# Attention and feed-forward kernel: input kept in the output sums, last two pairs plain, first products by 128 tokens

## The chip, the cores and the metric

The kernel runs on one core of one Trainium2 chip. The metric is the device time in microseconds; a run's time is compared with the median of the kernel's runs. TensorE (PE in the profile) does the matrix products, with its weight loads listed apart as PEld; VectorE is DVE, ScalarE is ACT, GpSimd is POOL, and SyncE (SP) issues all DMA transfers from one queue.

## The reference

One layer on 1024 tokens of width 512, in float32: attention with 32 heads of width 128 and a causal mask, then a feed-forward part of three square layers whose weights are signs (+1 or -1), each after a normalisation and each added to its input.

```python
x = x + attn(layernorm(x), wq, wkv, wo)
x = x + ffn(layernorm(x), k0, s0, k1, s1, k2, s2)

# attn: S = 1024, H = 32, DN = DV = 128, DQ = 192
q = (y @ wq).reshape(S, H, DQ)[..., :DN]
k = (y @ wkv)[:, : H * DN];  v = (y @ wkv)[:, H * DN : 2 * H * DN]   # by heads
scores = where(causal, q @ k.T * DQ ** -0.5, -1e30)
out = (softmax(scores) @ v).reshape(S, H * DV) @ wo

# ffn, D = 512, ei(y) scales the last fifth of y by -4 before the product
h = 2 * relu(s0 * (x @ sign(k0)))
h = 2 * relu(s1 * (ei(h) @ sign(k1)))
out = s2 * (ei(h) @ sign(k2))
```

## The kernel before, in words

**Layout.** Tokens lie in 8 tiles of 128 (`NT`), four to a half (`TPB`, halves of 512 tokens). The normalised input is transposed into `xnT` (features by tokens) by TensorE (`transposed`, L209, tile `ptx_a`), one tile after the other: statistics (L193, L194), square root on ScalarE (L196), reciprocal (L198), normalisation on VectorE (L203), four transposes, copy on ScalarE (L216).

**Pairs.** The 32 heads go in 16 pairs (`g`, 0 to 15). Every matmul but the transposes is recorded at L66, so this text tells them apart by the tile that they write. The projections of a pair and the output products are done in seven products of half-size blocks instead of eight (a Strassen scheme): `products` makes q, k and v of a pair in the banks `X`, `Y` and `Z`, from token sums `T` (`token_sums`, L229 to L232) and weight sums that POOL makes (`sums_of`, L244 to L247). Only q and k of pair 0 are made plainly, by `qk_plain`, at the start: for each half of the tokens, for q and k and both heads, four matmuls of 512 columns into one bank, copied out by ScalarE (L273).

**Heads.** For each query tile (`qt`, here "step"), `probabilities` makes the scores (`sc_qt`, one bank pair, so a score waits until the one before it has been read), VectorE takes the maximum and adds the mask (L465), ScalarE the exponential (L476), VectorE the reciprocal of the sum (L480), ScalarE the scaling (L481). The probabilities are transposed in two parts: VectorE transposes 32x32 blocks into `tb` (L487), and `exchange` moves the blocks by DMA into `pT` (L531: 16 transfers of 64 KB for the early block, query tiles 0 to 3, and 32 for the late block, tiles 4 to 7). `attend` then multiplies with v (`ps_av`) and copies the result to `attn` (L566). For the last head TensorE transposes instead (`ps_pT`, L515, copies at L518 and L520), and its query tiles run in the order 4 to 7, 0 to 3.

**Output products.** `o_products(g - 1)` runs during pair `g`: seven products of two halves each (14 units, each of two 256-column matmuls into a `ps_o` bank and one addition by VectorE into the seven sums `acc`, L411). The sums of all pairs but the last collect there. At the end `add_products` combines them into `x_out`, a second load of the input (L420 and L423, on VectorE and POOL):

```python
        into(nc.vector, 4, 0)
        to(nc.gpsimd, 0, 0, 0)
        into(nc.vector, 2, 4)
```

The last pair is plain: `o_unit` makes the output of one token tile with two 512-column matmuls and adds it to `x_out` (L448).

**Order.** The main loop goes over the 256 steps (`s` counts the 16 steps of a pair) and writes the order of TensorE out: after each step's scores it takes units from the chain of `products` and from the output's chain as long as shares of the pair's columns say so, and the matmuls are pinned in that order except in the first products and the last head, where a scheduler places them. Loads of weights stand at fixed steps. All DMA issues go through SP in order, and at most eight are under way.

**End.** The feed-forward part normalises `x_out` (`transposed_input`, tile `ptx_f`), splits it into a high and a low part, and runs `hidden_layer` and `output_layer`; the sign weights are made by POOL (L184). Its tiles lie in space of earlier stages: `acc`, `T`, `wraw`, `wv`, `pT`.

Of the kernel before, what the change touches and what calls it, by code (L numbers as in the profile page):

```python
# [29 lines left out]
def kernel(  # L30
# [54 lines left out]
    def load_x(tag, name):  # L85
        xt = const.tile([P, NT, D], F32, tag=tag, name=name)
        for t in range(NT):
            nc.sync.dma_start(xt[:, t, :], x_v[:, t, :])
        return xt

    x_in = load_x("acc", "x_in")
# [28 lines left out]
    w_raw, w_sum, wv_sb, wo_sb = {}, {}, {}, {}  # L120

    def load_qk_weights(which, g):
        w = pairs.tile([P, G, NC, DN], F32, tag="wraw", name=f"w{'qk'[which]}{g}")
        for i in range(G):
            h = g * G + i
            if which == 0:
                src = wq_v[:, :, h, :DN]
            else:
                src = wkv_v[:, :, h * DN : (h + 1) * DN]
            nc.sync.dma_start(w[:, i, :, :], src)  # L130
        w_raw[which, g] = w

# [5 lines left out]
    def load_o_weights(g):  # L138
        wo_sb[g] = pairs.tile([P, G, D], F32, tag="wo", name=f"wo{g}", bufs=1)
        nc.sync.dma_start(wo_sb[g], wo_v[:, g * G : (g + 1) * G, :])  # L140

    load_qk_weights(0, 0)
    load_qk_weights(1, 0)
    load_v_weights(0)
    load_o_weights(0)
    load_qk_weights(0, 1)

# [39 lines left out]
    def statistics(tiles, name):  # L187

        n = len(tiles)
        mv = small.tile([P, n, 2], F32, tag=f"mv{n}", name=f"mv_{name}")  # L190
        for t, xt in enumerate(tiles):
            stats = small.tile([P, 6], F32, tag="stats", name=f"stats_{name}{t}")
            nc.vector.bn_stats(stats, xt)  # L193
            nc.vector.bn_aggr(mv[:, t, :], stats)  # L194
        std = small.tile([P, n, 1], F32, tag=f"std{n}", name=f"std_{name}")
        nc.scalar.activation(std, mv[:, :, 1:2], AF.Sqrt, bias=eps)  # L196
        rstd = small.tile([P, n, 1], F32, tag=f"rstd{n}", name=f"rstd_{name}")
        nc.vector.reciprocal(rstd, std)  # L198
        return [(mv[:, t, 0:1], rstd[:, t, :]) for t in range(n)]

    def normalise(xt, mean_rstd, name):
        xn = work.tile([P, D], F32, tag="p", name=f"xn_{name}")
        nc.vector.tensor_scalar(xn, xt, *mean_rstd, ALU.subtract, ALU.mult)  # L203
        return xn
# [8 lines left out]
    for t in range(NT):  # L213
        stats = statistics([x_in[:, t, :]], f"a{t}")
        xn = normalise(x_in[:, t, :], stats[0], f"a{t}")
        nc.scalar.copy(xnT[:, :, t * P : (t + 1) * P], transposed(t, xn, "a"))  # L216
# [47 lines left out]
    def qk_plain(which, h, half):  # L264
        dst = (qT, kT)[which][h] if half else new_qk(which, h)
        w = w_raw[which, h // G][:, h % G]
        cols = slice(half * QB, (half + 1) * QB)
        ps = ps_mm.tile([P, QB], F32, tag="mm", name=f"ps_{'qk'[which]}{h}_{half}")
        for c in range(NC):
            matmul(  # L270
                ps, lhsT=w[:, c, :], rhs=xnT[:, c, cols], start=(c == 0), stop=(c == NC - 1)
            )
        nc.scalar.activation(dst[:, cols], ps, AF.Copy, scale=(-scale, 1.0)[which])  # L273
# [86 lines left out]
    acc = const.tile([P, 7, TPB, DH], F32, tag="acc", name="acc")  # L360
# [20 lines left out]
    def o_products(g):  # L381
# [8 lines left out]
        for m, left, right in (  # L390
            (0, lambda: attn[g * G, 0], a(0, 0)),
            (1, lambda: attn[g * G + 1, 0], a(0, 1)),
            (3, lambda: a_sum[g][0], s[0]),
            (2, lambda: a_sum[g][2], s[2]),
            (4, lambda: a_sum[g][1], s[1]),
            (5, lambda: a_sum[g][3], a(1, 1)),
            (6, lambda: attn[g * G + 1, 1], s[3]),
        ):
            left = left()
            for half in range(2):  # L400
# [7 lines left out]
                if g == 0:  # L408
                    nc.vector.tensor_copy(dst, ps)
                else:  # L410
                    nc.vector.tensor_tensor(dst, dst, ps, ALU.add)  # L411
                yield

    def add_products(xt):

        def to(eng, d, k, m):
            dst = xt[:, k * TPB : (k + 1) * TPB, d * DH : (d + 1) * DH]
            eng.tensor_tensor(dst, dst, acc[:, m], ALU.add)  # L420

        def into(eng, m, other):
            eng.tensor_tensor(acc[:, m], acc[:, m], acc[:, other], ALU.add)  # L423

        into(nc.vector, 4, 0)
        to(nc.gpsimd, 0, 0, 0)
        into(nc.vector, 2, 4)
        to(nc.gpsimd, 0, 0, 1)
        into(nc.vector, 4, 3)
        into(nc.gpsimd, 5, 2)  # L430
        into(nc.vector, 6, 4)
        to(nc.vector, 0, 1, 6)
        to(nc.gpsimd, 1, 0, 5)
        into(nc.vector, 3, 2)
        to(nc.vector, 1, 1, 3)

    def o_unit(g, t):
        ps = ps_mm.tile([P, D], F32, tag="mm", name=f"ps_o{g}_{t}")
        k, i = divmod(t, TPB)
        for j in range(G):  # L440
            matmul(
                ps,
                lhsT=attn[g * G + j, k][:, i * P : (i + 1) * P],
                rhs=wo_sb[g][:, j, :],
                start=(j == 0),
                stop=(j == G - 1),
            )
# [90 lines left out]
    def attend(h, qb, pieces):  # L538
        g, j = divmod(h, G)
        attn[h, qb] = const.tile([P, QB], F32, tag=f"attn{j}{qb}", name=f"attn{h}_{qb}")  # L540
# [26 lines left out]
        if qb == 1 and g + 1 < NG:  # L567
            attn_sums(g, early=(j == 0))

    for half in range(NQB):  # L570
        for which in range(2):
            for h in range(G):
                qk_plain(which, h, half)
# [35 lines left out]
    for i, (h, qt) in enumerate(steps):  # L609
# [3 lines left out]
        if s == 0:  # L613
            n_chain = 21 if g + 1 < NG else 7
            n_out = 14 if g > 0 else 0
# [4 lines left out]
                + O_PART * n_out  # L620
            )
            chain_end = 14 if g + 1 < NG else 6
        if s == 0:
# [3 lines left out]
            if g > 1:  # L627
                load_o_weights(g - 1)
        if s == 2:
            if g + 1 < NG:  # L630
                load_qk_weights(1, g + 1)
            if g > 0:
                o_chain = o_products(g - 1)
        if s == 6 and g + 1 < NG:
            weight_sums(1, g + 1)
        if s == 6 and g + 1 == NG:
            x_out = load_x("xnT", "x_out")
            xs = [x_out[:, t, :] for t in range(NT)]
        if s == 7 and g + 1 < NG:
            load_v_weights(g + 1)  # L640
        if s == 12:
# [4 lines left out]
            if g + 1 == NG:  # L646
# [11 lines left out]
        while True:  # L658
            want_chain = chain_done < min(n_chain, n_chain * (s + 1) / chain_end)
            want_out = s >= 2 and out_done < min(n_out, n_out * (s - 1) / 14)  # L660
# [4 lines left out]
            elif want_out and (done < goal or out_done + 2 < n_out * (s - 1) / 14):  # L665
                next(o_chain)
                out_done += 1
                done += O_PART
# [5 lines left out]
        if not late:  # L674
            attend(*to_attend.pop(i))
        if h == H - 1:
            if qt == 7:
                for _ in o_chain:
                    out_done += 1
                add_products(x_out)  # L680
# [5 lines left out]
        if h == H - 1 and s == NT:  # L686
            big = const.tile([P, 6, D], F32R, tag="T", name="w_signs")
            for n, (k, slots) in enumerate(
                ((k0, ("wraw", "wraw")), (k1, (0, 2)), (k2, (4, "wv")))
            ):  # L690
                chunks = []
                for m, slot in enumerate(slots):
                    if isinstance(slot, int):
                        w = big[:, slot : slot + 2, :]
                    else:
                        w = pairs.tile(
                            [P, 2, D],
                            F32R,
                            tag=slot,
                            name=f"w_sign{n}_{m}",  # L700
                            bufs=1 if slot == "wv" else None,
                        )
                    chunks += [w[:, 0, :], w[:, 1, :]]
# [5 lines left out]
    ff = const.tile([P, 7, NC // 2, QB], F32R, tag="acc", name="ff")  # L709

    def ff_part(n):
        return ff[:, 2 * n : 2 * n + 2].rearrange("p a b q -> p (a b) q")

    x_parts, h1, h2 = {}, {}, {}
    x_parts[1] = h2[1] = (ff_part(0), ff_part(1))
    h1[1] = (ff_part(2), pairs.tile([P, NC, QB], F32R, tag="pT", name="h1_lo1", bufs=3))
# [23 lines left out]
    def hidden_layer(i, k, src, dst):  # L740
        hi, lo = dst
        for oc in range(NC):
            ps = ffn_bank(f"ps_h{i}_{k}_{oc}")
            for c in range(NC):
                for part in range(2):
# [3 lines left out]
                        rhs=src[part][:, c, :],  # L749
                        start=(c == 0 and part == 0),  # L750
                        stop=(c == NC - 1 and part == 1),
# [3 lines left out]
            nc.vector.tensor_copy(hi[:, oc, :], h)  # L755
            nc.vector.tensor_tensor(lo[:, oc, :], h, hi[:, oc, :].bitcast(F32), ALU.subtract)

    def output_layer(k):
        for t in range(k * TPB, (k + 1) * TPB):
            ps = ffn_bank(f"ps_out{t}")  # L760
            cols = slice((t % TPB) * P, (t % TPB + 1) * P)
            for c in range(NC):
                for part in range(2):
                    matmul(
                        ps,
                        lhsT=h2[k][part][:, c, cols],
                        rhs=w_sign[2][c],
                        start=(c == 0 and part == 0),
                        stop=(c == NC - 1 and part == 1),
                    )  # L770
            osb = work.tile([P, D], F32, tag="p", name=f"osb{t}")
            nc.vector.scalar_tensor_tensor(osb, ps, s_sb[:, 2:3], xs[t], ALU.mult, ALU.add)
# [4 lines left out]
    for t in range(TPB):  # L777
# [4 lines left out]
    h1[0] = (  # L782
        pairs.tile([P, NC, QB], F32R, tag="pT", name="h1_hi0", bufs=3),
        keep.tile([P, NC, QB], F32R, tag="tb0", name="h1_lo0"),
    )
# [42 lines left out]
```

## Time and profile before

| what | value |
|---|---|
| median of 3 runs | 1373.1 us (1372.69 to 1373.99) |
| the profiled execution's time | 1373.51 us |
| its span, first to last instruction | 1371.5 us |
| TensorE busy | 1345.1 us, 98% |
| VectorE, ScalarE, POOL busy | 809.3, 495.8, 283.7 us |
| mean granted TensorE clock | 0.996 |

All runs lie within 0.1%. The span is 2.0 us shorter than the time of the same execution. Times in the order of time are counted from the first instruction. A row of the order of time has the start, the time until the end of the last of its instructions, the engine, the line, the operation with its tiles and shapes, the count, and in brackets the idle time before it with what ended it. A float32 matmul shows as two matmul records.

### The profile page before, as it was taken

What the parts mean: (1) busy time and instruction counts of PE and PEld (TensorE: products, weight loads), DVE (VectorE), ACT (ScalarE), POOL (GpSimd) and SP (SyncE); (2) the same over time, 40 slices, a digit from 0 to 9 for tenths busy, and PEclk for the clock granted to TensorE, in tenths of its full rate; (3) what the DMA queues carried; (4) which work ended last, traced back from release to release, by engine and by line L of the source; (5) the groups of instructions that cost most, each with busy time, mean ns of one, the idle gap of its engine ahead of it and who ended that gap; (6) DMA issues with size and microseconds to landing.
All of it is one profiled execution on the core that took longest, in us unless ns stands there. A gap on an engine that the chain in (4) does not pass through costs nothing.

```text
span 1371.5 us, 16621 instructions
## 1 busy us (share of the span) xinstructions
PE 1345.1 (98%) x5396; PEld 859.7 (63%) x5396; DVE 809.3 (59%) x1656; ACT 495.8 (36%) x921; POOL 283.7 (21%) x337
## 2 busy tenths in 40 slices
PE   7999999999999999999999999999999999999898
PEld 4646575665757566575756657575665757566467
DVE  3455565655656565655656565565656566556775
ACT  3444333333433333343333333333333333334222
POOL 5201222211222221121222112122211212212400
PEclk9999999999999999999999999999999999999999
DMA  4234344444444444444434444444444434335301
GB/s 123 64 96 114 96 104 112 113 103 106 107 99 110 106 112 102 106 109 100 113 99 115 102 102 114 100 108 103 114 103 99 119 96 112 99 90 146 85 1 62
DMA packets 266421, 139.31 MB, mean 102 GB/s; under 512 B 26208, under 2 KB 259168, under 8 KB 266336
## 3 DMA queue, kind: packets, MB, share of 16 engines
q1 hardware_dynamic: 266336, 138.25, 39.7%
q8 instruction: 44, 0.72, 0.2%
q14 instruction: 41, 0.34, 0.1%
HBM read 38.54 MB, written 2.10 MB: 30 GB/s over the span
## 4 chain that ended last, share of the span: by engine, by line
PE 94%; SPq 2%; DVE 2%; issue 1%; DMA 0%; ACT 0%; DVEq 0%; ACTq 0%
PE sc L66 17%; PE ps_av L66 17%; PE ps_o L66 14%; PE Y_v L66 6%; PE Y_q L66 6%; PE Y_k L66 5%; PE X_v L66 4%; PE Z_v L66 4%; PE X_q L66 4%; PE Z_q L66 4%; PE Z_k L66 4%; PE X_k L66 4%; PE ps_h L66 2%; SPq L531 2%; PE ps_out L66 1%; PE ps_q L66 1%
## 5 line engine op out<-in xcount | busy, mean ns | idle before, releaser
L476 ACT ACTIVATE p<-p,nmax 128x128 f32<-128x128 f32 (+7 forms) x256 | 198.3, 775 | 672.0 <-DVE nmax L465 670.0
L66 PE MATMUL sc<-kT,qT 128*128 128x512 f32 (+3 forms) x768 | 290.6, 487 | 4.8 <-DVE nmax L465 4.8
L465 DVE CUSTOM_DVE_ANT_0 p<-sc,mask 128x128 f32<-128x128 f32 (+7 forms) x256 | 191.4, 748 | 106.8 <-PE sc L66 106.6
L66 PE MATMUL ps_av<-pT,v 128*128 128x512 f32 x744 | 253.1, 490 | 0.6 <-DMA pT<-tb 0.6
L487 DVE STREAM_TRANSPOSE tb<-p 128x128 f32<-128x128 f32 (+1 forms) x248 | 187.0, 769 | 82.2 <-ACT p L481 78.7
L481 ACT ACTIVATE p<-p,rtotal 128x128 f32<-128x128 f32 (+7 forms) x256 | 196.1, 772 | 95.8 <-DVE rtotal L480 95.8
L66 PEld LDWEIGHTS ps_av<-pT,v 128*128 128x128 f32 x744 | 142.4, 192 | 129.1 <-issue 102.7
L66 PEld LDWEIGHTS sc<-kT,qT 128*128 128x128 f32 x768 | 140.3, 191 | 93.6 <-issue 77.1
L411 DVE TENSOR_TENSOR acc<-acc,ps_o 128x512 f32<-128x512 f32 x196 | 132.5, 682 | 56.6 <-PE ps_o L66 50.8
L480 DVE RECIPROCAL rtotal<-total 128x1 f32<-128x1 f32 x256 | 40.5, 158 | 112.9 <-ACT p L476 112.9
L66 PE MATMUL ps_o<-wo,attn 128*128 128x256 f32 (+1 forms) x392 | 104.3, 397 | 0.8 <-DVE attn L566 0.8
L372 POOL TENSOR_TENSOR at<-attn,attn 128x512 f32<-128x512 f32 x15 | 19.0, 1269 | 373.5 <-DVE attn L566 373.5
L66 PEld LDWEIGHTS ps_o<-wo,attn 128*128 128x128 f32 x392 | 70.9, 190 | 27.6 <-issue 21.0
L244 POOL TENSOR_TENSOR wsumk<-wk 128x256 f32<-128x256 f32 x15 | 10.9, 729 | 312.5 <-DMA wk<-in_L_attn_wkv_dram 296.9
L66 PEld LDWEIGHTS X_v<-wv,xnT 128*128 128x128 f32 x512 | 62.5, 192 | 5.2
L566 DVE COPY attn<-ps_av 128x512 f32<-128x512 f32 x62 | 42.3, 682 | 35.1 <-PE ps_av L66 34.5
L66 PE MATMUL X_v<-wv,xnT 128*128 128x128 f32 x512 | 62.5, 275 | 0.0
L66 PEld LDWEIGHTS ps_o<-osum,at 128*128 128x128 f32 x240 | 45.3, 190 | 23.9 <-issue 20.1
L66 PE MATMUL ps_o<-osum,at 128*128 128x256 f32 x240 | 59.3, 379 | 0.0
L66 PE MATMUL X_q<-xnT,wq 128*128 128x512 f32 x120 | 56.4, 592 | 0.0
L66 PE MATMUL X_k<-xnT,wk 128*128 128x512 f32 x120 | 56.4, 592 | 0.0
L476 ACT ACTIVATION_READ_ACCUMULATOR p<-p,nmax 128x1 f32 x256 | 47.8, 187 | 0.0
(160 smaller groups left out, 1643.6 us busy)
## 6 DMA issues: line engine op xcount, KB each, us to landing
pT<-tb SPq DMA_DIRECT2D x1488, 64.0 KB, 2.0
wq<-in_L_attn_wq_dram SPq DMA_DIRECT2D x32, 256.0 KB, 3.3
wk<-in_L_attn_wkv_dram SPq DMA_DIRECT2D x32, 256.0 KB, 3.7
wv<-in_L_attn_wkv_dram SPq DMA_DIRECT2D x16, 512.0 KB, 4.0
wo<-in_L_attn_wo_dram SPq DMA_DIRECT2D x16, 512.0 KB, 3.8
x_in<-_attn_hidden_states_dram SPq DMA_DIRECT2D x8, 256.0 KB, 4.5
x_out<-_attn_hidden_states_dram SPq DMA_DIRECT2D x8, 256.0 KB, 4.7
out_dram<-osb SPq DMA_DIRECT2D x8, 256.0 KB, 2.0
```

Of the source, the lines that this page charges most:

```text
L66: ins = nc.tensor.matmul(*args, **kw)
L244: nc.gpsimd.tensor_tensor(t[:, 0], a(1, 0), a(1, 1), ALU.add)
L372: nc.gpsimd.tensor_tensor(t0, b(0, 1), b(0, 0), ALU.subtract)
L411: nc.vector.tensor_tensor(dst, dst, ps, ALU.add)
L465: nc.vector.tensor_tensor_reduce(out=p[:, :n], in0=sc[:, :n], in1=mask[:, S - n :], scale=1.0, scalar=BIG, op0=ALU.add, op1=ALU.min, accum ...
L476: nc.scalar.activation(p[:, :n], p[:, :n], AF.Exp, bias=nmax, scale=-1.0, accum_out=total)
L480: nc.vector.reciprocal(rtotal, total)
L481: nc.scalar.activation(p[:, :n], p[:, :n], AF.Copy, scale=rtotal)
L487: nc.vector.transpose(tb[qb][:, : qt + 1, :, i, :], p[:, :n].rearrange("p (c b k) -> p c b k", b=NB, k=B32))
L531: nc.sync.dma_start(pT[b * B32 : (b + 1) * B32, :, a, :, :], tb[qb][a * B32 : (a + 1) * B32, chunks, b, :, :],)
L566: nc.vector.tensor_copy(dst.rearrange("p (t a i) -> p a t i", a=NB, i=B32), ps)
```

## The change

- **Input.** The input is loaded twice at the start: into `x_in`, two tiles in the space of `pT`, and again into four of the seven sums of `acc`, so that the sums of the output products start from it. POOL subtracts one sum from another once. `x_out` and its load are gone; `xs`, what the end reads and adds to, are parts of `acc`, in two pieces of 256 columns.
- **Weights between input tiles.** SP's first loads alternate: input tile 0, wq of head 0, tile 1, wq of head 1, tile 2, wk of head 0, tile 3, wk of head 1, tiles 4 to 7, then wv, wq of pair 1, wo, the second load of the input.
- **First products by 128 tokens.** `qk_plain` makes all four outputs (q and k of two heads) for one token tile after the other, in 128-column matmuls, in three banks of the `st` kind and the bank of the scores.
- **Combining.** The sums are numbered anew. `add_products` is seven additions `acc += acc` by VectorE, taken two a step from step 12 of pair 14 on. The output products of pair 13 are brought forward in pair 14 to be done by then (`out_by`).
- **Last two pairs plain.** Pair 14's output goes through `o_unit` as well, eight units from step 8 of pair 15 on. Its attention needs no sums any more. wo of pair 14 is loaded in pair 14, that of pair 15 at step 7 of pair 15, into the space of wv.
- **Space of the end.** Sign weights now lie in `xnT` and `T`, the parts of the feed-forward input in `pT`, `wraw`, `tb0` and `qT`. Statistics of a tile in two pieces take two `bn_stats` of 256 columns.

```diff
+    for t in range(NT):
+        load_x(t)
+        if t < TPB:
+            load_qk_weights(t // G, 0, [t % G])
...
-    load_qk_weights(0, 0)
-    load_qk_weights(1, 0)
     load_v_weights(0)
+    load_qk_weights(0, 1)
     load_o_weights(0)
-    load_qk_weights(0, 1)
+    acc = const.tile([P, 7, TPB, DH], F32, tag="acc", name="acc")
+    xs = []
+    for t in range(NT):
+        k, i = divmod(t, TPB)
+        xs.append(acc[:, 2 * k : 2 * k + 2, i, :])
+        nc.sync.dma_start(xs[t], x_v[:, t, :].rearrange("p (h d) -> p h d", h=2))
+
+    nc.gpsimd.tensor_tensor(acc[:, 2], acc[:, 2], acc[:, 3], ALU.subtract)
...
+                stats = small.tile([P, 2, 6], F32, tag="stats2", name=f"stats_{name}{t}")
+                for half in range(2):
+                    nc.vector.bn_stats(stats[:, half, :], xt[:, half, :])
...
-    def qk_plain(which, h, half):
...
+    def qk_plain(k):
+        outs = [(which, h) for which in range(2) for h in range(G)]
...
+        banks = [ps_st.tile([P, QB], F32, tag="st", name=f"ps_qk{k}_{n}") for n in range(3)]
+        banks.append(ps_sc.tile([P, S], F32, tag="sc", name=f"ps_qk{k}_3")[:, :QB])
+        for t in range(TPB):
+            tok = slice(t * P, (t + 1) * P)
+            for (which, h), ps in zip(outs, banks):
+                for c in range(NC):
+                    matmul(
+                        ps[:, tok],
+                        lhsT=w_raw[which, 0][:, h, c, :],
+                        rhs=xnT[:, c, k * QB + t * P : k * QB + (t + 1) * P],
...
-            (0, lambda: attn[g * G, 0], a(0, 0)),
-            (1, lambda: attn[g * G + 1, 0], a(0, 1)),
+            (4, lambda: attn[g * G, 0], a(0, 0)),
+            (0, lambda: attn[g * G + 1, 0], a(0, 1)),
...
-                if g == 0:
+                if g == 0 and m >= TPB:
                     nc.vector.tensor_copy(dst, ps)
...
+    def add_products():
+        for m, other in ((0, 4), (5, 4), (6, 5), (1, 6), (2, 3), (2, 5), (3, 6)):
+            nc.vector.tensor_tensor(acc[:, m], acc[:, m], acc[:, other], ALU.add)
+            yield
...
-        if qb == 1 and g + 1 < NG:
+        if qb == 1 and g + 2 < NG:
             attn_sums(g, early=(j == 0))
...
+            if g + 2 < NG:
+                out_by = [max(0, (14 * (t - 2) + 12) // 13) for t in range(G * NT)]
+            elif g + 2 == NG:
+                out_by = [0, 0, 0, 2, 4, 6, 6, 8, 10, 12, 13, 14, 14, 14, 14, 14]
+            else:
+                out_by = [max(0, t - NT + 1) for t in range(G * NT)]
...
-            if g > 0:
+            if g > 0 and g + 1 < NG:
                 o_chain = o_products(g - 1)
+            elif g > 0:
+                o_chain = (o_unit(g - 1, t) for t in range(NT))
...
-        if s == 6 and g + 1 == NG:
-            x_out = load_x("xnT", "x_out")
-            xs = [x_out[:, t, :] for t in range(NT)]
...
+        if g + 2 == NG and s >= 12:
+            if s == 12:
+                sum_chain = add_products()
+            for _ in range(2):
+                next(sum_chain, None)
         if h == H - 1:
-            if qt == 7:
-                for _ in o_chain:
-                    out_done += 1
-                add_products(x_out)
```

## The prediction

> **What bounds the kernel now.** I read the page's busy times first, then the busy times by stage, then the order of time on TensorE, VectorE and the DMA queue at both ends.
>
> ```profile
> PE 1345.1 (98%) x5396; PEld 859.7 (63%) x5396; DVE 809.3 (59%) x1656; ACT 495.8 (36%) x921; POOL 283.7 (21%) x337
> ```
>
> ```profile
> 0.00:44.00 44.00, 34.51 (x98) 18.67 (x98) 10.99 (x36) 12.00 (x25) 22.89 (x29) 1.00 0.36 108
> 193.00:270.00 77.00, 77.00 (x300) 48.18 (x299) 45.94 (x93) 27.84 (x51) 13.93 (x17) 1.00 0.44 109
> 1254.50:1312.00 57.50, 47.31 (x168) 27.80 (x168) 41.73 (x76) 18.83 (x37) 21.19 (x18) 0.94 0.37 103
> 1312.00:1345.00 33.00, 32.42 (x142) 23.77 (x141) 25.31 (x50) 11.99 (x20) 0.00 (x0) 1.00 0.00 1
> ```
>
> Columns: stretch, length, busy us of PE, PEld, DVE, ACT, POOL, granted clock, DMA share, GB/s. In the middle (a pair of heads takes 77 us) TensorE never rests, so an edit there counts only by its matmul columns. TensorE stands 9.5 us before 44 us and 10.2 us in the last head's stretch, 1254.5 to 1312, where the mean clock is 0.94 too. Those two stretches are what the change works on. The start, in order of time:
>
> ```profile
> 12.23 4.03 PE L209 MATMUL ptx_a<-ident,xn_a 128*128 128x128 f32 x20 [1.34 <-DVE rstd_a L198]
> 16.10 7.03 PE L66 MATMUL ps_q<-xnT,wq 128*128 128x512 f32 x16
> 43.57 0.38 PE L66 MATMUL sc<-kT,qT 128*128 128x128 f32 x2
> 44.88 1.95 PE L66 MATMUL X_v<-wv,xnT 128*128 128x128 f32 x16
> 46.66 1.95 PE L66 MATMUL Y_v<-wsumv,T 128*128 128x128 f32 x16
> ```
>
> The last head, TensorE and then VectorE:
>
> ```profile
> 1283.07 0.44 PE L515 MATMUL ps_pT<-ident,p 128*128 128x128 f32 x2 [1.34 <-ACT p L481]
> 1290.97 1.12 PE L66 MATMUL sc<-kT,qT 128*128 128x512 f32 x2 [2.08 <-DVE nmax L465]
> 1295.52 1.11 PE L515 MATMUL ps_pT<-ident,p 128*128 128x128 f32 x4 [2.06 <-ACT p L481]
> 1311.64 1.63 PE L209 MATMUL ptx_f<-ident,xn_f 128*128 128x128 f32 x12 [1.52 <-DVE xn_f L203]
> ```
>
> ```profile
> 1279.16 3.24 DVE L423 TENSOR_TENSOR acc<-acc 128x1024 f32<-128x1024 f32 x1
> 1282.43 4.39 DVE L423 TENSOR_TENSOR acc<-acc 128x1024 f32<-128x1024 f32 x2
> 1286.75 2.76 DVE L420 TENSOR_TENSOR x_out<-x_out,acc 128x1024 f32<-128x1024 f32 x2
> ```
>
> The sums of `add_products` hold VectorE from 1277 to 1289.5, the maximum of query tile 2 waits behind them, and TensorE behind that. The third resource is SP's queue of exchanges:
>
> ```profile
> 1224.37 32.83 SPq L531 DMA_DIRECT2D pT<-tb  x48
> 1257.31 3.90 SPq L88 DMA_DIRECT2D x_out<-_attn_hidden_states_dram  x8
> ```
>
> 48 exchanges (a head's second block and the next head's first) take 32.8 us of issue, about as long as a head's matmuls.
>
> **The start: later, +2.0 us.** The first products have the same 16,384 columns. A 512-column matmul costs 6.87/8 = 0.859 us (ps_q to ps_k), a 128-column one (46.66-44.88)/8 = 0.223, so 128 of them take 28.6 us for 27.5: +1.1 if nothing else moved. By the Trainium skill, "TensorE: Matmul & The Clock Gate", section Back-to-back issue gap, a sustained stream runs at about 81 ns for 128 columns and 131 for 512; 4 x 81/131 is 2.5 times the price, an estimate of +40 us. X_v is the same form on this chip and the row decides.
>
> What could be won is the wait for the last tile. The compiled order of TensorE, however, puts all transposes of tiles 0 to 7 in with only 7 products ahead of the last transpose; the queue is in order, so 121 products follow tile 7. And tile 7 is late: weights now go between the input tiles. The first twelve 256 KB loads landed at 3.4, 4.1, 5.8, 6.6, 7.1, 8.0, 9.0, 9.9, 10.7, 11.7, 12.5 and 13.4 (issue plus time to landing). The input was the first eight; now it is numbers 1, 3, 5, 7 and 9 to 12, so tile 4 comes at 10.7 and tile 7 at 13.4 instead of 9.9. From 10.7 VectorE has four statistics (0.63 each), five normalisations (0.54) and the small ones between (about 1.0): 6.2, to 16.9; it ended at 14.8. Last transposes 17.0 to 17.7, products 121 x 0.223 = 27.0, to 44.7. Then a new wait: the fourth product uses the bank of the scores, so sc_0 stands behind its copy, 0.60 and two handovers, 0.85: 45.5 against 43.57. Bounds: 0.0 if the tiles land in time and the transposes start as before, 2.7 if VectorE sees each landing late. I take 2.0.
>
> Hidden here: the second load of the input (8 issues of 0.46 on SP, behind wo; first used 70 us later), the POOL subtraction (2.35 by L229; POOL idles 13 us there). wq of pair 1 is released some 7 us later, as all tiles read wq0; its sums go from 40.7 to about 48, and Y_q reads them at 64.5: 16 us of cover.
>
> **Pairs 1 to 13: nothing.** The same columns, the products' order changed, the first one step later; VectorE has 31 us idle of 77. If that cover went, each late 0.69 add would be paid.
>
> **Pair 14, and what fills TensorE: +0.2.** Its products for pair 13 come earlier, and 7 sums `acc += acc` go on VectorE in the last four steps, 1.22 each alone (8.5 us). Walking those steps by the rows, they fit between maxima, except the fifth, which holds sc_6 for 0.2 us. The first maximum behind them is the one that would pay.
>
> **Pair 15 before the last head: waits for exchanges.** All fillers of pair 14's output leave the first half (4 of 0.86), and eight plain units of 4 x 0.43 = 1.72 come in the second: 13.8 for 12.0, +1.7 of work. I count from sc_7 of head 29, at 1216.96 before. Ahead of it three more units (2.6) are done and one k product (1.72) is not: +0.86. From there the matmuls to the second half of head 29's late block add to 27.6. The exchange before started 7.4 after sc_7 and its 32nd load landed at 29.4: TensorE, which came at 31.8, will now wait 1.8. The next 16 land at 41.6 (the 48th issue at 1256.6 and 2.0); head 30's early block is wanted at 40.2: it waits 1.4. So that block starts at 41.5 whatever happens between, in absolute time 1216.96 + 0.86 + 0.2 + 41.5 = 1259.5. If the queue's two long issues (1 us each) fall elsewhere, 1.4 less.
>
> Those waits can cost clock. After waits of 1.42 and 0.64 near 106 us the granted clock was 0.73 over 106 to 110; after 0.92 and 0.82 near 1258 it stayed 1.00. One stretch of 3.4 us at half speed costs 1.7, partly inside the second wait; the waits now are of about the length of those two pairs, so I add 0.3, a chance of one in five, with bounds 0 and 1.7. The same page, section What's actually happening, has the clock fall only after an idle window of about 3.4 us; by that these waits cost 0.
>
> **The last head: dense.** From that block to the first `ptx_f`: two blocks of 2.15, two of 5.58, scores 5.4, 31 transposes of 0.11 (3.4), 8 + 4 units of 1.72 (20.6): 44.9. I walked VectorE and ScalarE beside it: each maximum, exponential and scaling is ready 0 to 0.5 ahead of its transpose now, since 12 us of sums are gone; for the places with no margin I add 0.5. The wait ahead of `ptx_f` stays, 1.55: attention copy, reciprocal, normalisation. Statistics are now two of 256 columns; no row shows one (0.16 for an aggregate and 0.69 for 512 bound it); 0.40 makes +0.1 on the last tile, bounds -0.4 and +0.7. `ptx_f` starts at 1259.5 + 44.9 + 1.55 + 0.5 + 0.1 + 0.3 of clock = 1306.85 against 1311.64: -4.8. The clock of 0.5 that 1294 to 1298 had goes with the waits.
>
> **After that: nothing.** TensorE runs through the feed-forward part; the sign weights come from POOL some 5 us sooner and nobody waited. The output's reads of x have the same size in another layout.
>
> Sum: +2.0 and -4.8 is **-2.8**: span 1368.7, profiled time 1370.7 (2.0 lies around the span). The median was 0.4 below the profiled 1373.5, so **1370.3**. A measurement of this kernel tells 0.2%, 2.7 us, from no change.
>
> **Rivals.** *Input in time:* VectorE was not waiting for tiles 3 to 7 before; if it absorbs the new order and the exchange's long issues fall late, 2.0 and 1.4 are saved: 1366.9. For it: POOL and ACT waits that overlap; against: landing times. *Slower, sums ahead of the exchange:* where POOL ran beside them an `acc += acc` took 2.2 (4.39 for two). At that price 7 sums add 6.9 us to VectorE ahead of the transposes that start SP's exchanges; pair 15 runs at the pace of that queue, so all of it comes through once the slack of those steps, some 4 us, is used: with maxima held up in those steps about 5, ending at 1375.3. It decides from 1.8 us a sum. Against: POOL is busy only 3 us there. *Waits only move:* the last head stays as loose as before because scaling waits behind copies on ACT; 5 us of the 10.2 remain and the end is 1373.
>
> **Chances.** Forecast 0.42 (own range 1368.5 to 1372, about half of it beyond 0.2%), input in time 0.26, waits only move 0.12, slower 0.20. Faster 0.48, same 0.32, slower 0.20. The range, 1366.2 to 1375.0, reaches past the first rival and nearly to the slower one, and leaves out about a tenth at each end.
>
> **What would show it.** Right: sc_0 at 45 to 46, last `ptx_a` near 17; a wait for pT of 1 to 3 us in head 29's late block; under 4 us idle in the last head; `ptx_f` 4 to 6 us after its old place less the start's loss. Wrong: sc_0 before 43.5, sums of 2 us in pair 14, or waits for ACT in the last head as long as before.

## The result and the profile after

| kernel | median (runs) | range |
|---|---|---|
| before | 1373.5 us (14) | 1372.4 to 1374.2 |
| changed | 1371.2 us (14) | 1369.1 to 1375.1 |

The ratio is 0.9987, with a 95% interval of 0.9978 to 0.9997: faster by 0.4 to 3.0 us, and the 1.8 us of the ratio are less than the 2.7 us that this measurement can tell from no change. The changed kernel's times are wider apart and go with its granted clock: five runs at 1.000 took 1369.5 to 1370.9, four at 0.996 took 1374.5 to 1375.1, and the profiled execution is one of those (1375.12 us, span 1373.3). Its trace is therefore read by stages, and beside the traces of the experiments.

The page's busy times, and the busy times by stage of the changed kernel (columns as before: stretch, length, PE, PEld, DVE, ACT, POOL, clock, DMA share, GB/s):

```profile
PE 1349.3 (98%) x5564; PEld 872.3 (64%) x5564; DVE 803.3 (58%) x1658; ACT 495.9 (36%) x921; POOL 267.9 (20%) x326
```

```profile
0.00:47.25 47.25, 37.06 (x289) 35.53 (x289) 12.05 (x35) 12.45 (x26) 23.78 (x26) 1.00 0.45 141
200.00:277.00 77.00, 77.00 (x299) 48.14 (x298) 46.30 (x93) 27.48 (x50) 13.98 (x17) 1.00 0.44 110
1254.00:1258.00 4.00, 3.62 (x7) 1.99 (x8) 2.70 (x3) 0.00 (x0) 0.00 (x0) 0.57 0.41 98
1258.00:1314.00 56.00, 52.81 (x181) 27.87 (x180) 30.59 (x73) 19.09 (x37) 7.37 (x12) 1.00 0.28 73
```

The middle is as full as it was. In the last head TensorE stood 10.2 us of 57.5 before and now stands 3.2 of 56. The third line is a half-speed stretch that was not there before. The start, on TensorE in order of time:

```profile
15.15 2.34 PE L66 MATMUL ps_qk<-xnT,wq 128*128 128x128 f32 x10
17.28 1.60 PE L229 MATMUL ptx_a<-ident,xn_a 128*128 128x128 f32 x8
18.94 0.60 PE L229 MATMUL ptx_a<-ident,xn_a 128*128 128x128 f32 x4
44.61 1.95 PE L66 MATMUL ps_qk<-xnT,wk 128*128 128x128 f32 x16
47.25 0.49 PE L66 MATMUL sc<-kT,qT 128*128 128x128 f32 x2 [0.69 <-ACT kT L306]
```

The last transposes stand at 18.94 and the first score at 47.25, where it stood at 43.57. The first row shows why more was lost than late tiles: ten records took 2.34 us, 0.23 each, where sixteen take 1.95 later (0.12 each). The granted clock reads 1.00 all through this stretch, so it names no cause for the slow pace. Then pair 1's wait for its exchange, which was 0.64, and the last pair:

```profile
112.05 4.61 PE L66 MATMUL ps_av<-pT,v 128*128 128x512 f32 x8 [2.21 <-DMA pT<-tb]
...
1254.38 3.92 PE L66 MATMUL ps_av<-pT,v 128*128 128x512 f32 x8 [2.37 <-DMA pT<-tb]
1263.81 1.56 PE L66 MATMUL sc<-kT,qT 128*128 128x512 f32 x4 [0.93 <-DVE nmax L485]
1266.18 0.77 PE L535 MATMUL ps_pT<-ident,p 128*128 128x128 f32 x5 [0.81 <-ACT p L501]
1313.82 1.63 PE L229 MATMUL ptx_f<-ident,xn_f 128*128 128x128 f32 x12 [1.45 <-DVE xn_f L223]
```

Between 1266 and `ptx_f` TensorE waits for nothing. The block at 1254.38 shows both costs of its wait: 2.37 us idle, then 3.92 us for eight records that take 2.4 at full clock. On VectorE the sums in pair 14 cost 1.22 to 1.25 us each; one of them:

```profile
1217.00 1.22 DVE L454 TENSOR_TENSOR acc<-acc 128x1024 f32<-128x1024 f32 x1
```

Three lengths make every kernel here comparable: the start of the first score (A), from there to the start of the last score of head 29 (B; at 1216.96 before and 1224.33 now), and from there to the first `ptx_f` (C). They are from each kernel's one profiled execution; a half-speed stretch in it adds about 1.7 us to the length in which it lies.

| kernel | A | B | C | median us | ratio to before, 95% |
|---|---|---|---|---|---|
| before | 43.6 | 1173.4 | 94.7 | 1373.5 | |
| changed | 47.3 | 1177.1 | 89.5 | 1371.2 | 0.9978 to 0.9997 |
| start_undone | 43.2 | 1174.3 | 89.8 | 1368.5 | 0.9957 to 0.9981 |
| order_undone | 45.8 | 1173.3 | 88.5 | 1368.8 | 0.9962 to 0.9983 |
| wide_products | 46.9 | 1172.6 | 89.6 | 1371.2 | 0.9980 to 0.9997 |
| sums_doubled | 46.3 | 1173.7 | 90.3 | 1371.9 | 0.9981 to 0.9998 |
| sums_late | 46.9 | 1176.4 | 89.4 | 1370.8 | 0.9972 to 0.9990 |
| late_sums_doubled | 46.6 | 1173.1 | 97.1 | 1378.0 | 1.0021 to 1.0046 |
| before_no_sums | 44.2 | 1171.6 | 90.2 | 1367.5 | 0.9946 to 0.9971 |
| before_no_pool | 44.2 | 1171.6 | 89.9 | 1367.4 | 0.9939 to 0.9963 |
| spread_pair0 | 44.6 | 1172.8 | 88.1 | 1368.4 | 0.9951 to 0.9975 |
| units_ahead | 44.4 | 1172.9 | 86.0 | 1365.2 | 0.9924 to 0.9949 |
| changed_units_ahead | 46.5 | 1173.3 | 86.0 | 1367.5 | 0.9949 to 0.9976 |

### The profile page after: what moved, and what is told of

Its sections match the earlier page's. It is cut to its first block, busy times and chain, and to the rows that moved or that the text cites. A ratio compares the mean times of both kernels' runs of the same rounds, so it can differ in the third digit from the quotient of the medians.

```text
span 1373.3 us, 16933 instructions
## 1 busy us (share of the span) xinstructions
PE 1349.3 (98%) x5564; PEld 872.3 (64%) x5564; DVE 803.3 (58%) x1658; ACT 495.9 (36%) x921; POOL 267.9 (20%) x326
## 4 chain that ended last, share of the span: by engine, by line
PE 94%; SPq 3%; DVE 1%; DMA 1%; ACT 0%; issue 0%; ACTq 0%
PE ps_av L66 18%; PE sc L66 17%; PE ps_o L66 14%; PE Y_v L66 6%; PE Y_q L66 5%; PE Y_k L66 5%; PE X_v L66 4%; PE Z_v L66 4%; PE X_q L66 4%; PE Z_q L66 4%; PE X_k L66 3%; PE Z_k L66 3%; SPq L551 3%; PE ps_qk L66 2%; PE ps_h L66 2%; PE ps_out L66 1%
## 5 line engine op out<-in xcount | busy, mean ns | idle before, releaser
L448 DVE TENSOR_TENSOR acc<-acc,ps_o 128x512 f32<-128x512 f32 x190 | 128.9, 683 | 56.1 <-PE ps_o L66 50.9
L66 PE MATMUL ps_o<-wo,attn 128*128 128x256 f32 (+1 forms) x400 | 111.1, 414 | 0.0
L409 POOL TENSOR_TENSOR at<-attn,attn 128x512 f32<-128x512 f32 x14 | 17.7, 1266 | 348.4 <-DVE attn L589 348.4
L66 PEld LDWEIGHTS ps_o<-osum,at 128*128 128x128 f32 x224 | 42.5, 190 | 22.8 <-issue 19.1
L66 PE MATMUL ps_o<-osum,at 128*128 128x256 f32 x224 | 55.0, 379 | 0.0
```

The source lines that it names most:

```text
L66: ins = nc.tensor.matmul(*args, **kw)
L409: nc.gpsimd.tensor_tensor(t0, b(0, 1), b(0, 0), ALU.subtract)
```

## The experiments

The first theory was that the tail won about 5 us and the start lost more than the forecast said. The rivals: the last two pairs swallow what the start loses; or the tail's gain is not that of the moved sums.

### The start, in parts

**start_undone**, the changed kernel with the start of before:

```diff
     for t in range(NT):
         load_x(t)
-        if t < TPB:
-            load_qk_weights(t // G, 0, [t % G])
+    load_qk_weights(0, 0)
+    load_qk_weights(1, 0)
...
-        qk_plain(half)
+        for which in range(2):
+            for h in range(G):
+                qk_plain(which, h, half)
```

> The whole start is put back (input tiles first, then wq and wk; the first products in 512 columns), all else as changed: the tail alone. Theory (the start loses 3.7 us, all of which reaches the end, and the tail gains about 5): first score at 43.5 to 43.8 us, the wait for pT in pair 1 back to about 0.6 us, ptx_f near 1308, time 1367 to 1368.5 (5 to 6 us under the kernel before). Rival (the last two pairs run at the pace of the exchanges and swallow what the start loses): first score as early, but 1370.5 to 1371.5, as the changed kernel.

Measured 1368.5 us: 2.7 under the changed kernel and 5.2 under the one before, `ptx_f` at 1307.35. The 1370.5 to 1371.5 of the rival, in which the last pairs swallow the start's loss, did not come. **order_undone** puts back the first half of that diff alone, **wide_products** the second alone.

> Only the order of the first loads is put back (input tiles first); first products by 128 tokens as changed. Theory (most of the start's loss is the late tiles, whose transposes and seven first products fall into the slow clock): transposes end near 16.1, 128 products of 0.223 (28.5) end at 44.7, 0.7 for the copy of the scores' bank: first score at 45.3 to 45.5, time about 1.9 under the changed kernel, 1369.3. Rival (the 128-column form costs it): first score at 47, time 1371.

> Only the first products are put back to 512 columns, order q and k and heads as before; weights still go between the input tiles. Theory: tile 7 is normalised at 17.5 as in the changed kernel, transposed at 18.2, then 32 products of 0.859 (27.5): first score at 45.7, no wait for a copy; time about 1.5 under the changed kernel, 1369.7. Rival (landing order costs nothing): first score at 43.6, 1367.5.

The first score stood at 45.78 and 46.88; the medians are 1368.8 and 1371.2. TensorE of order_undone, then of wide_products:

```profile
12.49 4.02 PE L229 MATMUL ptx_a<-ident,xn_a 128*128 128x128 f32 x20 [1.34 <-DVE rstd_a L217]
16.34 1.95 PE L66 MATMUL ps_qk<-xnT,wq 128*128 128x128 f32 x16
45.78 0.49 PE L66 MATMUL sc<-kT,qT 128*128 128x128 f32 x2 [0.69 <-ACT kT L306]
```

```profile
16.44 2.82 PE L229 MATMUL ptx_a<-ident,xn_a 128*128 128x128 f32 x12 [1.09 <-DVE rstd_a L217]
46.88 0.38 PE L66 MATMUL sc<-kT,qT 128*128 128x128 f32 x2
```

With the tiles first, the transposes end at 16.5 and the products follow at 0.223 us each, as forecast. With weights between the tiles, the last three tiles' transposes start at 16.44, after a wait, and take 2.82 us, where the same twelve took 1.63 in start_undone; the 512-column products then save nothing. The expectation for wide_products missed by 1.5, as it put the last transposes at 18.2 and full pace.

By the medians the order of the loads costs 2.4 to 2.7 us and the 128-column form 0 to 0.3. But runs of one of these kernels lie up to 7 us apart (order_undone: 1367.0 to 1374.4), so a difference of two such medians is uncertain by some 2 us. The first scores split the loss in another way. With the tiles first, the 128-column form comes later by 1.2 to 2.6 us (45.78 against 43.2 to 44.6 in the six profiles with the start of before); with weights between the tiles the form makes no difference (46.3 to 47.3 against 46.88). So the loss of the whole start is shown, and how it divides between order and form is not.

### The sums

**sums_doubled** doubles the suspected cost in pair 14:

```diff
             nc.vector.tensor_tensor(acc[:, m], acc[:, m], acc[:, other], ALU.add)
+            nc.vector.tensor_tensor(acc[:, m], acc[:, m], acc[:, other], ALU.add)
             yield
```

> Each of the seven additions that combine the sums is made twice (the output is then not the reference's). Theory (the additions fit between maxima with about 4 us of slack in the four steps): 8.5 us more of VectorE, of which about 4.5 reach TensorE: waits for nmax in pair 14's last steps of 4 to 5 us, time 1375 to 1376. Rival 1 (VectorE has cover enough there): 1371 to 1372. Rival 2 (no slack at all): 1379.

1371.9 us, which its interval does not part from the changed kernel, and in its trace TensorE has no wait from 1160 to 1250: some 8 us more of VectorE around those four steps reach nobody. The slack is not 4 us but at least 8. Then the sums were moved back to where they were before:

```diff
+        last_max[0] = nmax
...
-        if g + 2 == NG and s >= 12:
-            if s == 12:
-                sum_chain = add_products()
-            for _ in range(2):
-                next(sum_chain, None)
         if h == H - 1:
+            if qt == 7:
+                for m in (4, 3):
+                    nc.vector.tensor_tensor(
+                        acc[:, m, 0, 0:1], acc[:, m, 0, 0:1], last_max[0], ALU.add
+                    )
+                for _ in add_products():
+                    pass
```

> The changed kernel with only the seven additions moved back into the last head, behind the maximum of its query tile 0 (two one-column additions of that maximum tie them to the place; the sums then also hold plain units, so the output is not the reference's). Theory (the tail's gain is that VectorE has no sums in the last head): waits for nmax and for the scaled p come back, 4 to 6 us in all, from the second half of head 29's last score to ptx_f 93 to 95 us instead of 88.5 to 89.5, and half-speed stretches behind the waits: 1374.5 to 1376.5. Rival (the eight plain units fill TensorE whatever VectorE does): 1371 to 1372.

The theory fell: 1370.8 us, C 89.4 as in the changed kernel, and no wait came back. VectorE of sums_late, and TensorE's score behind it:

```profile
1281.78 6.89 DVE L454 TENSOR_TENSOR acc<-acc 128x1024 f32<-128x1024 f32 x6
1288.58 0.42 DVE L487 CUSTOM_DVE_ANT_0 p<-sc,mask 128x256 f32<-128x256 f32 x1
```

```profile
1289.52 0.81 PE L66 MATMUL sc<-kT,qT 128*128 128x384 f32 x2
```

The maximum of query tile 1 waits behind six sums and ends at 1289.0, and TensorE needs it at 1289.5, since 8 us of units and of the last head's `ps_av` stand between the score of that tile, at 1280.4, and the next. From the other side, the kernel before was run without its sums:

```diff
                 for _ in o_chain:
                     out_done += 1
-                add_products(x_out)
```

> The kernel before with the combining of the sums left out altogether (its output lacks the attention's share of fifteen pairs). Theory: VectorE's 12 us of sums are what makes the last head wait; without them TensorE's idle time there falls from 10 to about 4 us, the half-speed stretch near 1294 goes, ptx_f at 1305.5 to 1307, time 1368 to 1369.5, so that moving the sums alone would have brought the tail's gain. Rival (the last head lacks matmuls to fill it, which only the plain units bring): ptx_f later than 1309, time over 1371.

1367.5 us, 6 us under the kernel before. So the combining in the last head costs 6 us in the kernel before, and nothing in the changed one. A second theory had to hold both: it is not VectorE's sums but GpSimd beside them. **before_no_pool** takes out GpSimd's four operations and leaves VectorE's seven:

```diff
         into(nc.vector, 4, 0)
-        to(nc.gpsimd, 0, 0, 0)
         into(nc.vector, 2, 4)
-        to(nc.gpsimd, 0, 0, 1)
         into(nc.vector, 4, 3)
-        into(nc.gpsimd, 5, 2)
         into(nc.vector, 6, 4)
         to(nc.vector, 0, 1, 6)
-        to(nc.gpsimd, 1, 0, 5)
```

> The kernel before with only GpSimd's four operations of the combining left out (the output lacks what they add); VectorE's seven stay in the last head. Theory (VectorE's sums cost the last head because GpSimd runs beside them and in the chain: two took 4.39 us and one 3.24 where one alone takes 1.22): VectorE's sums take about 9 us instead of 12.5, the last head's wait for nmax of 2.08 us is halved, time 1369 to 1370.5. Rival (any 9 us of sums stall the last head, since no output product is left to fill TensorE behind them): 1372 to 1373.

1367.4 us: all that before_no_sums gave, with VectorE's sums still there. GpSimd in the kernel before; then VectorE in before_no_pool, in the same stretch; then its TensorE:

```profile
1278.98 2.34 POOL L423 TENSOR_TENSOR acc<-acc 128x1024 f32<-128x1024 f32 x1 [10.55 <-DVE acc L423]
1281.40 3.21 POOL L420 TENSOR_TENSOR x_out<-x_out,acc 128x1024 f32<-128x1024 f32 x1
```

```profile
1277.98 1.22 DVE L423 TENSOR_TENSOR acc<-acc 128x1024 f32<-128x1024 f32 x1
1279.24 2.36 DVE L423 TENSOR_TENSOR acc<-acc 128x1024 f32<-128x1024 f32 x2
1281.52 2.35 DVE L420 TENSOR_TENSOR x_out<-x_out,acc 128x1024 f32<-128x1024 f32 x2
```

```profile
1285.98 1.02 PE L66 MATMUL sc<-kT,qT 128*128 128x512 f32 x2
1289.60 0.66 PE L511 MATMUL ps_pT<-ident,p 128*128 128x128 f32 x4 [2.13 <-ACT p L477]
1305.71 1.63 PE L209 MATMUL ptx_f<-ident,xn_f 128*128 128x128 f32 x12 [1.52 <-DVE xn_f L203]
```

The same five operations took 1.22, 2.36 and 2.35 without GpSimd and 3.24, 4.39 and 2.76 beside it (the last two beside its work on the sign weights): 4.5 us of stretching, without idle time of VectorE between them. In the kernel before, the maximum behind them came 4.5 us late, and TensorE's clock halved for twice 3.4 us in the waits that followed. In before_no_pool the wait of 2.08 for that maximum is gone, the one for a scaled `p` stays (2.13), and the clock halved once. C is 4.8 us shorter than before, not 6.6 as the median: B is shorter by 1.8 too, since the profile of the kernel before has a half-speed stretch from 107.8 on and this one has none. Nothing shows that the four operations, over a thousand us later, have to do with that.

The rival that any sums stall an empty last head would have had 1372. TensorE's idle time from the last head's first score to `ptx_f` is 10.2 us before, 6.8 without any sums, 6.4 without GpSimd's and 3.2 in the changed kernel: GpSimd explains a little over half of the fall. The rest came with the denser last head of the changed kernel, whose plain units no run took out by themselves.

**late_sums_doubled**, sums_late with each addition made twice, tells how much cover there was:

> As sums_late, with each of the seven additions made twice, 16 to 17 us of VectorE in the last head (output not the reference's). Theory (in sums_late VectorE came free 0.9 us before TensorE needed the next maximum, so the cover of the plain units was used up): the second 8 us reach TensorE almost whole, waits for nmax and p of 6 to 8 us, time 1377 to 1379. Rival (there is cover left): 1371 to 1373.

1378.0 us, 7.2 more than sums_late (C 97.1 for 89.4). Its TensorE:

```profile
1291.56 1.65 PE L66 MATMUL sc<-kT,qT 128*128 128x384 f32 x2 [5.34 <-DVE nmax L488]
```

The cover in the last head is the half microsecond seen above; a second 8 us show up almost whole, in a wait of 5.34 and a half-speed stretch of 6.8 that begins in it.

### The exchanges and the first pair

**units_ahead**, on top of start_undone, brings two plain units ahead of head 29's late block:

```diff
-                out_by = [max(0, t - NT + 1) for t in range(G * NT)]
+                out_by = [0, 0, 0, 1, 2, 2, 2, 2, 2, 2, 3, 4, 5, 6, 7, 8]
...
-            elif want_out and (done < goal or out_done + 2 < out_by[s] or g + 2 == NG):
+            elif want_out and (done < goal or out_done + 2 < out_by[s] or g + 2 >= NG):
```

> As start_undone, with two of pair 14's eight plain units brought forward to steps 3 and 4 of pair 15, ahead of head 29's late block. Theory (pair 15 runs at the pace of the exchanges): the wait of 3.2 us for pT in head 29's late block goes to under 0.5, and head 30's early block, which starts 42.5 us after head 29's last score whatever lies between, waits 2 to 3 us instead; time as start_undone, 1368 to 1369. Rival (the wait is saved, since the next block's exchange is early enough): 1365 to 1366.

The rival won: 1365.2 us, 3.4 under start_undone. TensorE of start_undone, then of units_ahead:

```profile
1248.39 2.39 PE L66 MATMUL ps_av<-pT,v 128*128 128x512 f32 x8 [3.19 <-DMA pT<-tb]
...
1260.24 2.40 PE L66 MATMUL ps_av<-pT,v 128*128 128x512 f32 x8 [0.80 <-issue]
```

```profile
1244.82 5.75 PE L66 MATMUL ps_av<-pT,v 128*128 128x512 f32 x16
1258.46 0.77 PE L517 MATMUL ps_pT<-ident,p 128*128 128x128 f32 x5 [0.82 <-ACT p L483]
1261.35 2.40 PE L66 MATMUL ps_av<-pT,v 128*128 128x512 f32 x8
```

SP's exchanges for the two blocks, in the same order:

```profile
1224.79 33.33 SPq L533 DMA_DIRECT2D pT<-tb  x48
```

```profile
1224.57 32.12 SPq L533 DMA_DIRECT2D pT<-tb  x48
```

Head 29's block runs through with no wait, and head 30's early block, at 1261.35, finds its data there: the last issue ends at 1256.7. In start_undone it ends at 1258.1, and the block starts 2.1 us later, about the 2.0 that such a load takes to land. Counted from head 29's last score it starts 1.3 us later than in start_undone, but 3.4 us of units are done by then. On the changed kernel with its own start the same edit gives as much:

> The changed kernel, start and all, with only two of pair 14's units brought ahead of head 29's late block. Theory (the wait of 2.4 us there and the half-speed stretch that follows it in some executions are both saved, whatever the start does): no wait for pT in pair 15, 3 to 4 us under the changed kernel, 1367 to 1368.5, and executions closer together. Rival (the start's delay uses up what the units bring): 1370 to 1371.

1367.5 us, 3.7 under the changed kernel. units_ahead is the fastest version here, 0.9937 of the kernel before.

**spread_pair0** tries the waits between pairs 0 and 1:

```diff
-            chain_end = 14 if g + 1 < NG else 6
+            chain_end = 6 if g + 1 == NG else 14 if g else 15
```

> As start_undone, with pair 0's 21 products spread over 15 steps instead of 14. Theory (in pair 0's last steps TensorE has no products left, so it waits 1.42 us for a maximum and 0.5 to 2.2 us for pT, and the clock halves for 3.4 us in some executions): the first wait goes, the granted clock stays 1.00 at 100 to 115 us, time 1.4 to 2.5 us under start_undone: 1366 to 1367. Rival (the exchange of pair 0's last block sets it, the wait only moves there): 1368.5, with a wait for pT of 1.9 or more.

1368.4 us: the wait of 1.42 for a maximum went and the one for pT became 2.33. Here the exchange does seem to set the time, as the rival said.

## Why the prediction was right and wrong

**The sum** was 1370.3 and the median 1371.2, inside the forecast's own range, but that it came so near is in part luck: the start was dearer, pair 1 has a wait that was not in the sum, the tail's price was right for a reason that did not hold, and the median depends on the granted clock of the executions. Of the signs of being right, two held (a wait for pT of 1 to 3 us, under 4 us idle in the last head) and two at the start failed (47.25 for 45 to 46, and 18.9 for 17).

**The start: mis-sized, +2.0 for +2.7** (1371.2 against start_undone's 1368.5; the first scores of the five profiles with this start and of the six with the other also lie 2.7 apart in the mean). The landing walk held: the last normalisation ended at 17.5 for a forecast 16.9, the 128-column products took 0.223 (128 of them are 28.5 us, where the working has 28.6), and the bank's copy cost 0.69 for 0.85. What failed is the pace between: the last transposes came at 18.9, not 17.0. The normalisation makes 0.6 of that; in the rest the five products of the row above and the transposes around them ran at about half pace, and I had priced them at the rate of the middle. The five profiles with this start took 1.7 to 2.3 us for these ten records and have the first score at 46.3 to 47.3. Why the pace is low there stays open.

**Pairs 1 to 13: nothing** missed one wait. For pT in pair 1 TensorE waits 1.0 to 2.2 us in all six profiles with the 128-token products and 0.5 to 0.75 in six with the 512-column ones (spread_pair0, whose edit lengthens it, left out). What in the new order brings it is not settled.

**Pair 14: right price, wrong slack.** Seven sums of 1.22 us. The slack was put at 4 us and is at least 8: doubled, the sums cost nothing that can be measured. So the slower rival had no place here.

**Pair 15: the wait was there (2.37 for 1.8, and 2.1 to 3.2 in the eight profiles with this pair 15), what follows from it was wrong.** The step that failed is "that block starts at 41.5 whatever happens between". It made the wait free, because the next block's exchange would catch TensorE anyway. The next exchange held TensorE by 0.8 us at most; with work put ahead the wait is saved, 3.4 to 3.7 us. The units' place, not the queue's pace, left it there.

**The last head: right size, wrong cause.** The idle time fell to 3.2 us and C by 5.2. But I gave this to "12 us of sums are gone". Sums of 8.5 us in the same place cost nothing, in the changed kernel (sums_late) as in the one before (before_no_pool). What cost there was the 4.5 us by which GpSimd stretched them, and the half-speed stretch behind that. The row of 4.39 us that I used for the slower rival's price was this cause; I didn't apply it to the place where it stood.

**Clock: too small.** I put a chance of one in five on one half-speed stretch. The profiled execution has three (two in a row from 110.6 on, one from 1254.0 on), and nine of the changed kernel's fourteen runs lie below a granted clock of 1.000. The profile of the kernel before has three as well (one from 107.8 on, two in a row from 1292 on), and none of its 54 runs beside the experiments lies above 0.998. At 0.996 the changed kernel took 1374.5 to 1375.1 and the one before 1372.4 to 1375.6. So the lower median rests on the executions with fewer such stretches. The sum had the last head's stretch go, rightly, but nothing for a second one in pair 1.

## What to carry to other kernels

Before moving an engine's work out of a tight stretch, look whether its instructions are longer there than elsewhere: here VectorE's additions cost nothing in the tight stretch once GpSimd's beside them were gone (before_no_pool leaves their work undone, sums_late has all of it on VectorE). A wait that looks free because a second limit is near should be tried by putting ready work ahead of it. Whatever is put between the first loads delays the first tiles, and products among the first transposes, before about 19 us, cost up to twice their later price here.

## What the runs showed of the hardware

**GpSimd and VectorE held each other up in additions of two SBUF operands.** A VectorE addition that began at 1279.16, 0.2 us after one of GpSimd's, took 3.24 us: 2.16 until GpSimd's end at 1281.32 and 1.1 more, about what it takes alone. GpSimd's next took 3.21 instead of 2.34, and the two of VectorE beside it 4.39 instead of 2.36. The Trainium skill, "SBUF — State Buffer", section Who interferes with whom, says that an instruction of VectorE with two SBUF inputs and one of GpSimd that reads SBUF contend for a shared interface. These rows agree.

**Half-speed stretches don't need an idle window of their length.** In these profiles they lasted 3.4 or 6.8 us. Busy times by stage of the changed kernel around its wait of 2.37 us, then of start_undone behind its wait of 3.19 (the eighth value is the granted clock):

```profile
1253.00:1254.00 1.00, 0.00 (x0) 0.00 (x0) 0.00 (x0) 0.00 (x0) 0.00 (x0) 1.00 0.47 112
1255.00:1256.00 1.00, 1.00 (x2) 0.34 (x1) 1.00 (x3) 0.00 (x0) 0.00 (x0) 0.50 0.45 108
```

```profile
1248.40:1252.00 3.60, 3.60 (x12) 2.09 (x13) 3.25 (x4) 0.00 (x0) 0.00 (x0) 1.00 0.44 105
```

The shorter wait cost the clock and the longer one did not (nor did one of 2.97 in wide_products), so the length of a wait alone does not decide.

The Trainium skill, "TensorE: Matmul & The Clock Gate", section What's actually happening, has a window of 3413 ns that runs freely, which agrees with the lengths and with executions that differ; its rule that the clock falls after an idle window of about 3.4 us does not cover the fall behind 2.37. In the 3.4 us ahead of that fall TensorE had been idle for about 2.0. What share of a window decides was not measured.
